# A three-stage layer kernel: the first wide layer as seven products of quarters, and both wide layers' weights loaded for every block

## The chip, the cores and the metric

The kernel runs on one core of one Trainium2 chip. The metric is the device time of one execution in microseconds (us), the median of three runs.

## What is computed

x has 4 sequences of 1024 tokens with 256 channels. Three sublayers follow each other, each of them behind a layer norm and added to its input: half a feed-forward net, a long convolution, and half the same feed-forward net again. Cut to what matters:

```python
def _L0_ffn_ref(x, w1_w, w1_s, w2_w, w2_s, h1_w, h1_s, h2_w, h2_s, w3_w, w3_s):
    h = silu(_tlin(x, w1_w, w1_s)) * _tlin(x, w2_w, w2_s)      # 256 -> 1024
    h = gelu(_tlin(h, h1_w, h1_s))                             # 1024 -> 1024, first wide layer
    h = gelu(_tlin(h, h2_w, h2_s))                             # 1024 -> 1024, second wide layer
    return _tlin(h, w3_w, w3_s)                                # 1024 -> 256
x = x + 0.5 * ffn(layernorm(x))
x = x + gelu(causal_convolution(layernorm(x), K)) @ W.T + b    # K: 1024 taps for each channel
x = x + 0.5 * ffn(layernorm(x))
```

`_tlin(x, w, s)` is x times the transpose of w, scaled by s for each output; all the weights w are -1, 0 or 1.

## The kernel before

**Blocks.** The 4096 tokens are cut into 8 blocks of 512. The feed-forward net runs over the 8 blocks as turn "f" (x to x1) and again as turn "g" (x2 to the output), 16 blocks in the order f0 to f7, g0 to g7. In between, the convolution takes each of the 4 sequences through `mix`, from x1 to x2. Activations lie with features on the 128 partitions and the block's 512 tokens along the free axis.

**Two parts.** Activations go to TensorE as fp32r in two parts, an upper part (a cast) and a lower part (value minus upper part), so each product is two matmuls. Weights are whole numbers and need one part. The program also looks at the weights on the chip (`weight_checks`, 44 pieces), and a second copy of the whole program in plain fp32 stands behind an `If` for weights that fp32r can't hold; it doesn't run here.

**A block's stages (`ffn`, L352).** First the narrow layer: for each of 8 groups of 128 features m, 4 matmuls for pa (w1) and 4 for pb (w2), then Silu on ScalarE (L362), the product on VectorE (L363), the cast on ScalarE (L367) and the low part on VectorE (`low_part`, L287). Then the two wide layers: for each m, 8 chunks k x 2 parts = 16 matmuls of 512 columns into one PSUM bank (`linear`, L344), Gelu (L377), cast (L379), low part (L287). Last, w3 with 32 matmuls: `last_squares` with an addition on GpSimd and stores by its queue, in the final block `last_tokens` (L423), whose 64 matmuls have 256 columns of w3 as the moving operand. A block has 352 fp32r matmuls, 256 of them in the wide layers.

**Buffers.** All weights are resident in SBUF; h1_sb and h2_sb take 32 KB of each partition each. The activations in two parts rotate through 15 "ring" buffers, other tiles of 512 columns through 19 "half" buffers, and all matmul results through 8 PSUM banks that share one tag.

**The order of the work.** A compile-time scheduler of the language sets each engine's order; the order of the code is the priority, and what is ready may go ahead. Convolution work is mixed into the blocks: `all_aside` is a generator for the kernel's taps, their spectrum and the four `mix`es, and after each m of a wide layer `tick` draws from it until about 2500 units are drawn, where a VectorE operation counts 130 plus its columns (L137). A generator step that yields PAUSE ends a tick, and where nothing is left, a tick takes a weight check instead. In parallel `ahead` steps `prepare` (L956), which loads, normalizes and transposes the next block. `spectrum` (L699) multiplies by trigonometric matrices that SP's queue loads (`matrix`, L713): products into PSUM, a copy by ScalarE (f_m, L731), sums and differences on VectorE. `mix` ends with the inverse (pi, L905), Gelu (yt) and the product with W (pw, L930).

**Queues.** At the start GpSimd's queue loads w1, w2, the tap parameters, h1, h2, the second block, w3 and the rest, in this order. SP's queue loads the first block, the constants, and later all that blocks and convolution read; GpSimd's stores.

Of the kernel before, what the change touches and what calls it, by code (L numbers as in the profile page):

```python
# [31 lines left out]
JQ = J // 2  # L32
N_WARM = 9


STEP_WORK, OP_WORK, MIN_WORK = 2500, 130, 300
PAUSE = "pause"
N_CHECKS = 44

# [58 lines left out]
def macaron_layers(  # L98
# [22 lines left out]

    nc = tc.nc
# [7 lines left out]
    psum = ctx.enter_context(tc.tile_pool(name="psum", bufs=8, space=bass.MemoryType.PSUM))  # L130

    work_done = 0
# [16 lines left out]
    def bank(name):  # L149
        return psum.tile([P, 512], F32, tag="ps", name=name)  # L150

    def half(name, *shape, dtype=F32):

        return work.tile([P, *(shape or (512,))], dtype, tag="half", name=name, bufs=19)

    def ring(name, *shape, dtype=F32):

        return work.tile([P, *shape], dtype, tag="ring", name=name, bufs=15)
# [9 lines left out]
    h1_sb = keep.tile([P, KH, HID], wide, name="h1_sb")  # L168
    h2_sb = keep.tile([P, KH, HID], wide, name="h2_sb")
# [12 lines left out]
    k_hat = dram.tile([2 + len(PAIRS), 2, P, 2, D], F32, name="k_hat")  # L182

# [37 lines left out]


# [21 lines left out]
    for t, src in ((h1_sb, h1), (h2_sb, h2)):  # L244
        for k in range(0, KH, 2):
            weights_from.dma_start(t[:, k : k + 2, :], rows(src)[:, k : k + 2, :])
# [42 lines left out]
    def transposed(xn, name):  # L289


        pts = [bank(f"pt_{name}_{k}") for k in range(DC)]
# [47 lines left out]
    def linear(ps, w, m, acts):  # L340
        n = len(acts)
        for k in range(n):
            for part in range(parts):
                nc.tensor.matmul(  # L344
                    ps,
                    w[:, k, m * P : (m + 1) * P],
                    acts[k][:, part, :],
                    start=(k == 0 and part == 0),
                    stop=(k == n - 1 and part == parts - 1),
                )  # L350

    def ffn(xt, src, dst, blk, name, tick, ahead, final):  # L352


        ha = []
        for m in range(KH):
            pa, pb = bank(f"pa_{name}_{m}"), bank(f"pb_{name}_{m}")
            linear(pa, w1_sb, m, xt)
            linear(pb, w2_sb, m, xt)
            g = half(f"g_{name}_{m}")  # L360
            t = ring(f"ha_{name}_{m}", parts, TB, dtype=wide)
# [4 lines left out]
            if split:  # L366
                nc.scalar.copy(t[:, 0, :], g)  # L367
                low_part(t, g)
            ha.append(t)
        for layer, w in ((2, h1_sb), (3, h2_sb)):  # L370
            hb = []
            for m in range(KH):
                ps = bank(f"p{layer}_{name}_{m}")
                linear(ps, w, m, ha)
                t = ring(f"h{layer}_{name}_{m}", parts, TB, dtype=wide)
                g = half(f"g{layer}_{name}_{m}") if split else t[:, 0, :]
                nc.scalar.activation(g, ps, AF.Gelu, scale=sc_sb[:, layer, m : m + 1])  # L377
                if split:
                    nc.scalar.copy(t[:, 0, :], g)  # L379
                    low_part(t, g)  # L380
                hb.append(t)
                ahead()
                if layer == 2 or m < KH - 1:
                    tick()
            ha = hb
# [3 lines left out]
        (last_tokens if final else last_squares)(ha, src, dst, blk, name)  # L389

    def last_squares(ha, src, dst, blk, name):
# [8 lines left out]
        for k in range(DC):  # L400
            ps = bank(f"po_{name}_{k}")
            linear(ps, w3_sb, k, ha)
# [7 lines left out]
    def last_tokens(ha, src, dst, blk, name):  # L410
# [7 lines left out]
        def result(ps, i, n):  # L418

            for e in range(n):  # L420
                for k in range(KH):
                    for part in range(parts):
                        nc.tensor.matmul(  # L423
                            ps[:, e * D : (e + 1) * D],
                            ha[k][:, part, (i + e) * P : (i + e + 1) * P],
# [18 lines left out]
        ps = bank(f"po_{name}_0")  # L444
# [3 lines left out]
        for e in range(2):  # L448
            ps = bank(f"po_{name}_{2 + e}")
# [5 lines left out]
    def weight_checks():  # L455

        todo = []
        for src, held in ((w1, w1_sb), (w2, w2_sb), (h1, h1_sb), (h2, h2_sb), (w3, w3_sb)):
            n_k, width = held.shape[1], held.shape[2]
            by = max(1, 512 // width)  # L460
            for k in range(0, n_k, by):
                for c in range(0, width, 512):
                    cols = slice(c, min(c + 512, width))
                    todo.append((rows(src)[:, k : k + by, cols], held[:, k : k + by, cols]))
        assert len(todo) == N_CHECKS

        def load(n):
            given = half(f"given_{n}", *todo[n][1].shape[1:])
# [5 lines left out]
        for n, (src, held) in enumerate(todo):  # L474
            given = following
            if n + 1 < len(todo):
                following = load(n + 1)
            stt(
                given,
                given,  # L480
                0.0,
                held.bitcast(F32),
                ALU.add,
                ALU.not_equal,
                accum_out=miss[:, n : n + 1],
            )
            yield

# [3 lines left out]
        nc.vector.tensor_reduce(total, miss[:, 0:N_CHECKS], axis=mybir.AxisListType.X, op=ALU.add)  # L492
        yield
        ps = psum.tile([1, 1], F32, tag="ps", name="p_bad")
# [109 lines left out]
    def kernel_steps():  # L604
# [7 lines left out]
        for g0 in range(0, DD, group):  # L612
# [34 lines left out]
            def products(d1, a):  # L647
# [3 lines left out]
                if at == 0:  # L651
                    pk = psum.tile([P, per_tile, 2, NB], F32, tag="ps", name=f"pk_{g0 + d1}")
# [46 lines left out]
    def spectrum(rows_of, name, over=1):  # L699
# [22 lines left out]
        def products(q, m):  # L722
            ps = []
            for e in range(2):
                ps.append(psum.tile([P, 2, D], F32, tag="ps", name=f"pf_{name}_{q}_{e}"))
# [17 lines left out]
        for n in (0, 2):  # L743
            qs = order[n : n + 2]
            if n == 0:
                for q, m in zip(qs, ms):
                    products(q, m)
                ms = [matrix(q) for q in order[2:4]]
                yield PAUSE
            for q in qs:  # L750
                sums(q)
            if n == 0:
# [369 lines left out]
```

## Time and profile before

| | |
|---|---|
| median of 3 runs | 1405.61 us (1404.97 to 1405.88) |
| profiled execution | 1405.23 us, its span 1403.3 us |
| granted TensorE clock | 0.999 |
| TensorE busy | 1393.0 us, 6492 matmul instructions |
| VectorE busy | 838.6 us (60%) |
| ScalarE busy | 707.6 us (50%), 51 table loads ahead of Gelu |
| DMA | 101.27 MB, mean 72 GB/s; 355 GB/s in the first 35 us |

In a group's line stand the line of the code, the engine, the operation, the written tile and those read, the shapes and the count; then the busy time and the mean time of one in ns, then the idle time ahead of it and what ended that. The timeline's lines begin with the start and the length in us. PEld is TensorE's weight load, which overlaps its matmuls. Two rows that the change touches:

```profile
L344 PE MATMUL p_g<-ha_g,h_sb 128*128 128x512 f32 x1024 | 236.2, 390 | 0.0
L287 DVE TENSOR_TENSOR h_g<-g_g,h_g 128x512 fp32r<-128x512 f32 x128 | 88.6, 692 | 249.6 <-ACT h_g L379 249.3
```

### The profile page before, as it was taken

How to read it: one execution, taken by the hardware profiler on the slowest of the kernel's cores; microseconds unless marked ns; L12 is line 12 of the kernel's file. 1: busy time of each engine (PE TensorE's matmuls, PEld its weight loads, DVE VectorE, ACT ScalarE, POOL GpSimd, SP SyncE). 2: the span in 40 equal slices, each digit the busy share in tenths (PEclk: the TensorE clock that was granted, in tenths of full speed). 3: DMA queues.
4: the chain of work that ended last, by engine and by line, in shares of the span. 5: the costliest groups of instructions: out<-in, count | busy, mean ns of one | idle time of the engine just before them, and what ended most of it. 6: DMA issues, size and time to landing. Idle time of an engine off the chain costs nothing.

```text
span 1403.3 us, 17882 instructions
## 1 busy us (share of the span) xinstructions
PE 1393.0 (99%) x6492; PEld 1161.4 (83%) x6492; DVE 838.6 (60%) x1614; ACT 707.6 (50%) x1070; POOL 266.3 (19%) x398
## 2 busy tenths in 40 slices
PE   8999999999999999999999999999999999999998
PEld 7888888888888888888888888888888888888887
DVE  6896567755547774387773568753566762542412
ACT  5986579644546344354352454533545342553532
POOL 4321012211312120320113201213112121121200
PEclk9999999999999999999999999999999999999999
DMA  9410101112231322422213404132223122511000
GB/s 355 117 20 26 35 16 46 30 48 77 67 96 30 113 71 73 136 60 84 61 53 113 113 31 138 20 97 74 86 70 82 43 63 98 135 22 39 15 16 19
DMA packets 111139, 101.27 MB, mean 72 GB/s; under 512 B 72304, under 2 KB 82544, under 8 KB 111040
## 3 DMA queue, kind: packets, MB, share of 16 engines
q1 hardware_dynamic: 93248, 55.37, 14.6%
q0 software_dynamic: 17520, 44.39, 11.1%
q8 instruction: 53, 0.87, 0.3%
q14 instruction: 46, 0.38, 0.1%
q10 hardware_dynamic: 272, 0.26, 0.1%
HBM read 76.91 MB, written 23.07 MB: 71 GB/s over the span
## 4 chain that ended last, share of the span: by engine, by line
PE 99%; DMA 1%; POOL 0%; DVE 0%; issue 0%; POOLq 0%
PE p_f L344 33%; PE p_g L344 33%; PE po_f L344 4%; PE pa_g L344 4%; PE pb_g L344 4%; PE pa_f L344 4%; PE pb_f L344 4%; PE po_g L344 4%; PE pi L905 2%; PE pf_m L727 2%; PE pw L930 2%; PE pk L654 1%; PE po_g L423 1%; DMA w_sb<-in_w_dram 1%; PE pf_k L727 0%; POOL w_sb L238 0%
## 5 line engine op out<-in xcount | busy, mean ns | idle before, releaser
L287 DVE TENSOR_TENSOR h_g<-g_g,h_g 128x512 fp32r<-128x512 f32 x128 | 88.6, 692 | 249.6 <-ACT h_g L379 249.3
L344 PE MATMUL p_f<-h_f,h_sb 128*128 128x512 f32 x1024 | 237.1, 391 | 0.0
L344 PE MATMUL p_g<-ha_g,h_sb 128*128 128x512 f32 x1024 | 236.2, 390 | 0.0
L344 PE MATMUL p_f<-ha_f,h_sb 128*128 128x512 f32 x1024 | 235.3, 390 | 0.0
L344 PE MATMUL p_g<-h_g,h_sb 128*128 128x512 f32 x1024 | 235.2, 390 | 0.0
L377 ACT ACTIVATE g_g<-p_g,sc_sb 128x512 f32<-128x512 f32 x128 | 88.2, 689 | 278.9 <-PE p_g L344 276.5
L344 PEld LDWEIGHTS p_g<-ha_g,h_sb 128*128 128x128 f32 x1024 | 192.1, 188 | 39.8
L344 PEld LDWEIGHTS p_g<-h_g,h_sb 128*128 128x128 f32 x1024 | 192.1, 188 | 39.8
L344 PEld LDWEIGHTS p_f<-h_f,h_sb 128*128 128x128 f32 x1024 | 191.8, 188 | 40.1 <-DVE h_f L287 0.3
L344 PEld LDWEIGHTS p_f<-ha_f,h_sb 128*128 128x128 f32 x1024 | 191.9, 188 | 39.8
L377 ACT ACTIVATE g_f<-p_f,sc_sb 128x512 f32<-128x512 f32 x128 | 87.7, 689 | 190.0 <-PE p_f L344 189.6
L287 DVE TENSOR_TENSOR h_f<-g_f,h_f 128x512 fp32r<-128x512 f32 x128 | 87.8, 690 | 149.0 <-ACT h_f L379 148.5
L317 POOL DMA_DIRECT2D moved<-sq_g x64 | 34.9, 552 | 330.3 <-DVE sq_g L140 290.7
L379 ACT CAST h_g<-g_g 128x512 fp32r<-128x512 f32 x128 | 79.3, 620 | 4.0
L379 ACT CAST h_f<-g_f 128x512 fp32r<-128x512 f32 x128 | 78.3, 618 | 2.9
L377 ACT ACT_TABLE_LOAD x51 | 65.4, 1283 | 26.0 <-PE p_f L344 14.3
L344 PE MATMUL pa_f<-xt_f,w_sb 128*128 128x512 f32 x256 | 69.0, 390 | 1.1 <-DVE xt_f L299 0.7
L344 PE MATMUL pb_f<-xt_f,w_sb 128*128 128x512 f32 x256 | 68.8, 389 | 0.0
L344 PE MATMUL pa_g<-xt_g,w_sb 128*128 128x512 f32 x256 | 68.4, 389 | 0.0
L344 PE MATMUL pb_g<-xt_g,w_sb 128*128 128x512 f32 x256 | 68.4, 389 | 0.0
L363 DVE SCALAR_TENSOR_TENSOR g_g<-pb_g,sc_sb,g_g 128x512 f32<-128x512 f32 x64 | 47.9, 749 | 31.5 <-PE pb_g L344 19.7
L317 POOL DMA_DIRECT2D moved<-sq_f x56 | 30.8, 556 | 181.2 <-DVE sq_f L140 181.2
(234 smaller groups left out, 1844.4 us busy)
## 6 DMA issues: line engine op xcount, KB each, us to landing
h_sb<-in_h_dram POOLq DMA_DIRECT2D x8, 1024.0 KB, 15.0
given<-in_h_dram SPq DMA_DIRECT2D x32, 256.0 KB, 3.6
kr<-k_hat SPq DMA_DIRECT2D x20, 256.0 KB, 2.6
ki<-k_hat SPq DMA_DIRECT2D x20, 256.0 KB, 2.8
xr_f<-in_x_dram SPq DMA_DIRECT2D x64, 64.0 KB, 2.4
x<-y_f POOLq DMA_DIRECT2D x64, 64.0 KB, 2.2
xm<-x SPq DMA_DIRECT2D x8, 512.0 KB, 3.7
m_m<-in_cosm_dram SPq DMA_DIRECT2D x16, 256.0 KB, 5.2
```

Of the source, the lines that this page charges most:

```text
L287: return nc.vector.tensor_tensor(t[:, 1, :], src, t[:, 0, :].bitcast(F32), ALU.subtract)
L317: stores.dma_start(moved[k].rearrange("(c r) a q -> a r c q", r=SQ)[a], sq[a * SQ : (a + 1) * SQ].rearrange("r c j s -> r c (j s)"),)
L344: nc.tensor.matmul(ps, w[:, k, m * P : (m + 1) * P], acts[k][:, part, :], start=(k == 0 and part == 0), stop=(k == n - 1 and part == parts ...
L363: nc.vector.scalar_tensor_tensor(g if split else t[:, 0, :], pb, sc_sb[:, 1, m : m + 1], g, ALU.mult, ALU.mult)
L377: nc.scalar.activation(g, ps, AF.Gelu, scale=sc_sb[:, layer, m : m + 1])
L379: nc.scalar.copy(t[:, 0, :], g)
L423: nc.tensor.matmul(ps[:, e * D : (e + 1) * D], ha[k][:, part, (i + e) * P : (i + e + 1) * P], w3_sb[:, k, :], start=(k == 0 and part == 0) ...
L654: nc.tensor.matmul(pk[0:NA, at + i, :, :].rearrange("p h b -> p (h b)"), a[:, i].rearrange("p a b -> p (a b)"), qd[d1 // per_tile][:, at + ...
L727: nc.tensor.matmul(ps[e][:, part, :], m[:, e, part, :], rows_of(q + JQ * e), start=True, stop=True)
L905: nc.tensor.matmul(banks[dc][e][:, q * P : (q + 1) * P], vs[q + JQ * e][:, part, dc * P : (dc + 1) * P], m[:, e, part, :], start=(part == ...
L930: nc.tensor.matmul(ps[:, e * D : (e + 1) * D], yts[dc][j // JQ][:, (j % JQ + e) * P : (j % JQ + e + 1) * P], wt_sb[:, dc, :], start=(dc == 0),
```

## The change

**Seven products.** In all blocks but f0, the first wide layer is computed as a two-by-two product of quarters: the weights in four quarters of 512 x 512 (A), the activations in four quarters of 512 features x 256 tokens (B), with seven products of quarters and sums of quarters (Winograd's form of Strassen's method) in place of eight. The sums of weights (S1, S2, S3, S4, -A22) are made once, during f0, and stored in DRAM beside A11 and A12. The sums of activations (t1 to t4), the additions of kept products (p1, p5, u2) and the low parts are VectorE's; casts, copies out of PSUM and Gelus are ScalarE's. A product is 32 matmuls of 256 columns over two PSUM banks.

**Weights in quarters.** h1_sb and h2_sb are gone. Four slots of 1 MB take quarters: seven for the first wide layer and four for the second, in every block, on SP's queue. h2 is copied from DRAM to DRAM at the start (and quarters A11 and A12 of h1), f0's h1 quarters come by GpSimd's queue.

**What goes with it.** PSUM is divided: six banks with tags of their own for the net, two for the convolution. Ring has 14 buffers, half 18. Ticks come in the narrow layer too (1700 units after every second m), after each bank of a product (600) and after each m of a plain wide layer (3100). `spectrum` goes through its four products one by one with a PAUSE each, its matrices loaded two ahead; the inverse does its two halves of two banks each with a PAUSE between. The checks of h1 and h2 take two VectorE passes each instead of one and look at the weights in DRAM.

```diff
+NARROW_WORK, SUMS_WORK, WIDE_WORK = 1700, 600, 3100
+ORDER = (A11, S1, A12, S2, S3, S4, MINUS_A22)
...
-    psum = ctx.enter_context(tc.tile_pool(name="psum", bufs=8, space=bass.MemoryType.PSUM))
+    psum = ctx.enter_context(tc.tile_pool(name="psum", bufs=1, space=bass.MemoryType.PSUM))
...
+    def piece(name, tag):
+        return work.tile([P, TB], F32, tag=tag, name=name, bufs=5)
...
+                t = work.tile([P, QK, QW], F32R, tag="slot", name=f"w_f0_0_{m}{k}", bufs=4)
+                weights_from.dma_start(t, quarter_of(h1, m, k))
+        nc.sync.dma_start(h2_raw, h2)
+        nc.sync.dma_start(quarters[A11], quarter_of(h1, 0, 0))
+        nc.sync.dma_start(quarters[A12], quarter_of(h1, 0, 1))
...
+            if split and m % 2 == 0:
+                tick(NARROW_WORK)
+        if by_sums:
+            acts = winograd(raw, name, tick, ahead)
+        for layer in (3,) if by_sums else (2, 3):
+            acts = plain(acts, layer, name, tick, ahead)
...
+    def operand(quarter, name):
+        ops = []
+        for p, src in enumerate(quarter):
+            t = ring(f"{name}_{p}", parts, TB, dtype=wide)
+            nc.scalar.copy(t[:, 0, :], src)
+            low_part(t, src)
+            ops.append(t)
+        return ops
...
+    def product(banks, weights, ops, step, first=True):
+        for p, ps in enumerate(banks):
+            for e in range(2):
+                m = 2 * p + e
+                for c in range(QK):
+                    for part in range(parts):
+                        nc.tensor.matmul(
+                            ps[:, e * QT : (e + 1) * QT],
+                            weights[:, c, m * P : (m + 1) * P],
+                            ops[c // 2][:, part, c % 2 * QT : (c % 2 + 1) * QT],
...
+            step()
...
+        def times(banks, ops, first):
+            product(banks, slots.pop(0), ops, step, first)
+            load_slot()
...
+        def plus(sums, banks):
+            for o, ps in zip(sums, banks):
+                nc.vector.tensor_tensor(o, ps, o, ALU.add)
+            return sums
+
+        def activated(k, n, quarter, into):
+            for p, (src, g) in enumerate(zip(quarter, into)):
+                for c in range(2):
+                    m = k * QK + 2 * p + c
+                    cols = slice(c * QT, (c + 1) * QT)
+                    nc.scalar.activation(
+                        g[:, cols], src[:, cols], AF.Gelu, scale=sc_sb[:, 2, m : m + 1]
+                    )
+                upper, lower = (t[:, :, n * QT : (n + 1) * QT] for t in out[2 * k + p])
+                g = g.rearrange("p (c t) -> p c t", c=2)
+                nc.scalar.copy(upper, g)
+                nc.vector.tensor_tensor(lower, g, upper.bitcast(F32), ALU.subtract)
+
+        b11 = operand(of(0, 0), named("b11"))
+        t1 = less(of(0, 1), of(0, 0), named("t1"))
+        t1_ops = operand(t1, named("t1s"))
+        times(pa, b11, True)
+        p1 = kept(pa, named("p1"))
+        t2 = less(of(1, 1), t1, named("t2"))
+        t2_ops = operand(t2, named("t2s"))
+        times(pd, t1_ops, True)
+        p5 = kept(pd, named("p5"))
+        b21 = operand(of(1, 0), named("b21"))
+        times(pa, t2_ops, False)
+        u2 = kept(pa, named("u2"))
+        t3 = less(of(1, 1), of(0, 1), named("t3"))
+        t3_ops = operand(t3, named("t3s"))
+        times(pe, b21, True)
+        activated(0, 0, plus(p1, pe), p1)
+        b22 = operand(of(1, 1), named("b22"))
+        times(pa, t3_ops, False)
+        activated(1, 1, plus(p5, pa), p5)
+        t4 = less(t2, of(1, 0), named("t4"))
+        t4_ops = operand(t4, named("t4s"))
+        times(pd, b22, False)
+        activated(0, 1, plus(u2, pd), u2)
+        times(pa, t4_ops, False)
+        activated(1, 0, pa, [piece(f"c21_{name}_{p}", "sum") for p in range(2)])
...
+        t = work.tile([P, QK, QW], F32R, tag="slot", name=name, bufs=4)
+
+        nc.sync.dma_start(t.bitcast(F32), src)
+        slots.append(t)
```

`less` makes two differences on VectorE ("diff" pieces), `kept` two copies out of PSUM on ScalarE ("sum" pieces), and `pa`, `pd`, `pe` are the net's bank pairs 4 and 5, 0 and 1, 2 and 3. `load_slot` fetches the next quarter in the order of use.

## The prediction

> **What bounds the kernel now.** I read the busy table and the chain that ended last first, then TensorE's groups by form, then one stage in the timeline.
>
> ```profile
> PE 1393.0 (99%) x6492; PEld 1161.4 (83%) x6492; DVE 838.6 (60%) x1614; ACT 707.6 (50%) x1070; POOL 266.3 (19%) x398
> ...
> PE 99%; DMA 1%; POOL 0%; DVE 0%; issue 0%; POOLq 0%
> PE p_f L344 33%; PE p_g L344 33%; PE po_f L344 4%; PE pa_g L344 4%; PE pb_g L344 4%; PE pa_f L344 4%; PE pb_f L344 4%; PE po_g L344 4%; PE pi L905 2%; PE pf_m L727 2%; PE pw L930 2%; PE pk L654 1%; PE po_g L423 1%; DMA w_sb<-in_w_dram 1%; PE pf_k L727 0%; POOL w_sb L238 0%
> ```
>
> TensorE is the whole chain, and the two wide layers (p_f, p_g) are two thirds of it. Its waits, listed, come to 3.9 us, all in the first 11 us. So time falls only if TensorE gets less work, and rises as soon as TensorE has to wait.
>
> What a matmul costs is read from start to start, since the ends overlap. TensorE's timeline, a whole wide layer and the last layer of the last block, and the weight loads of the latter:
>
> ```profile
> 715.76 29.18 PE L344 MATMUL p_g<-ha_g,h_sb 128*128 128x512 f32 x128
> 744.78 1.05 PE L905 MATMUL pi<-mi,v_False 128*128 128x128 f32 x8
> ```
> ```profile
> 1388.83 8.09 PE L423 MATMUL po_g<-w_sb,h_g 128*128 128x256 f32 x64
> 1391.14 5.57 PEld L423 LDWEIGHTS po_g<-w_sb,h_g 128*128 128x128 f32 x46 [0.20 <-DVE h_g L287]
> ```
>
> (744.78 - 715.76) / 128 = 226.7 ns for 512 columns. L423 is the only place where fp32r matmuls have 256 columns, each with its own weight load, and that is the form the change makes: the undisturbed 46 take (5.57 - 0.19) / 45 = 119.6 ns. That is 6 ns over half of 226.7: each matmul carries some 13 ns that don't shrink with its columns.
>
> **The products.** Per block, the first wide layer's 128 matmuls of 512 columns (29.02 us) become 7 products x 4 row groups x 4 chunks x 2 parts = 224 of 256 columns: 224 x 119.6 = 26.79 us. The saving is 2.23 us, not the eighth (3.63 us) that the algebra has. Block f0 keeps the old form, so 15 x 2.23 = **33.4 us** off the path.
>
> Here the Trainium skill ("TensorE: Matmul & The Clock Gate", section Back-to-back issue gap) is weighed. It puts a sustained stream of weight load and matmul at 81 ns for 128 columns and 131 ns for 512, which speaks against the change: between those, 256 columns would be about 98 ns (my interpolation), so 224 x 98 = 22.0 us against 128 x 131 = 16.8 us, a loss of 5.2 us a block and 78 in all. The trace excludes its 131: it has 226.7 here. Its formula for one isolated matmul, N/2.4 + 2.5 ns, gives 27.6 - 24.5 = 3.2 us a block, 47 in all. I take the rows of the trace, between the two.
>
> **VectorE.** Of the block's low-part subtractions, 16 fall away (8 ha_, 8 of the first wide layer). The sums bring 14 low parts of operands, 8 differences, 6 additions of kept products and 8 low parts of results: 36, net +20. All have forms the trace has:
>
> ```profile
> 728.83 0.68 DVE L140 TENSOR_TENSOR v_False<-u_i,w_i 128x512 f32<-128x512 f32 x1
> 729.43 0.68 DVE L140 TENSOR_TENSOR v_True<-u_i,w_i 128x512 f32<-128x512 f32 x1
> ```
>
> Each lasts 0.68 but the next starts after 0.60 us. So 36 x 0.60 = 21.6 us lie in the seven-product stage, where 8 low parts (4.8 us) lie today. Over the run: 15 x 20 x 0.60 = 180 us, plus 16 sums of weights (10 us), plus one more pass for each of 32 weight checks (19 us): 838.6 + 209 = 1048 us, some 75% of a span near 1386. By the average it is covered. By stage less so: the stage gets 14 ticks of 600 units of spectrum work; 642 units are one 512-column op of 0.60 us, so up to 7.9 us. 21.6 + 7.9 = 29.5 us of VectorE if the budget is used fully, 26.7 at the two thirds that I estimate (about 410 us of counted work against 16 x 37,500 units, 560 us), beside TensorE's 26.8 plus its own spectrum work. That (pf, pw, pi, pk: 28.9 + 28.9 + 33.8 + 16.4 = 108 us, 7 a block) gives the stage some 1.6 us. So 28.4 against 26.7 to 29.5: VectorE just fits, because the six ops for b11 and t1 (3.6 us) need only the first half of the narrow layer.
>
> They may run that early because engines don't follow the code's order:
>
> ```profile
> 704.18 0.75 DVE L363 SCALAR_TENSOR_TENSOR g_g<-pb_g,sc_sb,g_g 128x512 f32<-128x512 f32 x1 [1.29 <-ACT g_g L362]
> 705.16 0.75 DVE L363 SCALAR_TENSOR_TENSOR g_g<-pb_g,sc_sb,g_g 128x512 f32<-128x512 f32 x1 [0.23 <-PE pb_g L344]
> 705.83 1.71 DVE L287 TENSOR_TENSOR ha_g<-g_g,ha_g 128x512 fp32r<-128x512 f32 x2
> ```
>
> The code has product, low part, product, low part; the program has two products, then two low parts. What is ready goes first, so operands of later products fill gaps.
>
> **ScalarE** per block loses 16 casts (0.62 each) and 8 Gelus (0.69), 15.4 us; it gains 14 + 8 casts (13.6), 6 copies from PSUM (0.59, the row f_m: 3.5) and 16 Gelus of 256 columns (about 0.41, by the 256-column row k_minus: 6.6), 23.7 us. Net 8.3 x 15 = 125 us; 707.6 becomes 832, 60%. Hidden by the average.
>
> **The new waits.** Which comes last in the stage? The "sum" tag has five buffers; kept p1, p5 and u2 want six. So the second piece of u2 waits for p1's first piece, and product 5, which adds into u2's bank, waits for u2's copy. In us from the stage's start, at 3.83 a product: product 4's first bank ends at 13.4; 0.24 until another engine sees it (19.39 streamed, ScalarE at 19.63 in the 715.8 stage); addition 0.69; the Gelu table 1.28; two Gelus 0.82; cast 0.62; low part 0.69; copy 0.59: 18.3. Product 5's second bank wants to start at 17.2. TensorE would wait 1.1 us, more by each op queued ahead on two engines near 90% in this stage, less where product 6 (which needs none of this) or spectrum matmuls are placed in the gap. Bounds: 0 when filled; 2 to 4.5 us when ScalarE's order is late. I take 0.8: **15 x 0.8 = 12 us**. The other tight place, the second wide layer's start, needs product 6's results: addition, Gelus, cast, low part make 3.1 us after its last bank, and product 7 covers 3.83. Without that cover it costs up to 3.1 us a block.
>
> **Weights.** Each block now loads 11 quarters of 1 MB on SP's queue, where nothing was loaded: about 169 MB more. A slot is reused four products on, so a load has three products, 11.5 us. 256 KB land in 2.6 to 3.6 us and 512 KB (xm) in 3.7, so I estimate 5.5 for 1 MB. In the stage 7 MB in 28 us is 250 GB/s, beside 46 to 93 GB/s there now; the start shows 355 GB/s as what the engines move. Near full, but two of the seven aren't needed until the next layer's second half. Cost 0, bound 2 us a block. Queued behind a slot load that waits for TensorE are SP's loads for the spectrum (m, mi, xr, factors); the diff loads matrices two products ahead, so I take 0.
>
> **The start.** The first 35 us are already full:
>
> ```profile
> 0.00:35.00 35.00, 31.11 (x138) 25.80 (x139) 23.59 (x56) 19.45 (x30) 14.95 (x27) 1.00 1.10 355
> ```
>
> (TensorE, weight loads, VectorE, ScalarE, GpSimd, clock, DMA share, GB/s.) SP now copies 6 MB from DRAM to DRAM at once, beside w1 and w2, for which TensorE waits until 10.47. At half the bandwidth their second chunks, issued at 3.2 and landing after 7.2 us, would come up to 7 us later; the h1 quarters then still arrive in time at 7.2 us each. I take **4 us** (0 to 7). The weight sums (4 MB read, 5 written) come in f0's ticks and are due at its end: 0.
>
> **Other moves.** The spectrum's PSUM goes from eight shared banks to two: after each pair a copy (0.59) and two sums (1.2) must pass. Wide matmuls fill that, as the 64 pi matmuls lie between them today; 0, bound 1 us a block. h1_sb and h2_sb gone, 14 ring buffers in place of 15, GpSimd's extra 20 stores in f0: 0. The checks fit the ticks of the last blocks, where VectorE is 2 to 5 tenths busy.
>
> **Sum** against the profiled execution (1405.23 us; span 1403.3; median of the runs 1405.61, 0.03% away): 1405.2 - 33.4 + 12 + 4 = **1388 us**.
>
> **Rivals.**
> *Nothing waits:* 1405.2 - 33.4 + 4 = 1376. For it: 22 of the 36 sums make operands, which can be done early. Chance 0.13.
> *The stage turns on ScalarE and VectorE (slower).* From product 4's first bank to the next layer's start 13.4 us, ScalarE has three activations of 2.9 us, the table 1.28, the b22 and t4 casts and the u2 copy 3.1: 13.1 us. The next block's norm falls there (Sqrt 0.3 with its table, then Gelu's again: 2.9 us). That is 16.0, so products 5 to 7 come late. At 4.5 us a block: 1405.2 - 33.4 + 4 + 67.5 = 1443. It decides from (33.4 - 4) / 15 = 1.96 us a block. Against it: the norm and the b22 and t4 casts (2.5) can be drawn earlier. Chance 0.30.
> *256 columns cost more.* All 64 of L423 with its waits are 8.09 / 64 = 126 ns; then 28.3 us a product stage, 12 us saved, and 1409 with the costs above. Chance 0.08.
> *Even:* the quarters or half the late chain eat 2 us a block: 1405. Chance 0.07.
> *The forecast,* 1377 to 1401: 0.42.
>
> Faster by over 0.2% (2.8 us, about what a measurement can tell from no change): 0.42 + 0.13 = 0.55; within it 0.07; slower 0.38. The range leaves a tenth at each end: 1373 to 1442.
>
> **What would show it.** The product matmuls start 119 to 121 ns apart: the first step. VectorE near 75% overall, over 85% in the stage: the second. TensorE's waits before the products: 0.8 us a block on ScalarE's copy (u2) in products 5 or 6; if they name the b22 or t4 low parts or the outputs at the next layer's start, and sum to 30 us or more, the slower rival holds. Waits on the quarters' DMA prove my zero wrong. The first wide matmul after 24.2 tells the start.

## The result and the profile after

The change made the kernel slower: 1520.21 us (median of 4 runs, 1517.22 to 1523.28) against 1405.74 us; ratio 1.0815, 95% interval 1.0792 to 1.0838. The forecast was 1388 us. The profiled execution's span is 1519.2 us. Its page, in the lines that answer to those of before:

```profile
PE 1411.8 (93%) x7932; PEld 1231.3 (81%) x7932; DVE 1062.3 (70%) x1963; ACT 817.1 (54%) x1373; POOL 277.1 (18%) x414
...
PEclk7999999999999999999999999999999999999999
...
PE 42%; DVE 6%; DMA 3%; issue 1%; ACT 1%; SPq 0%; POOL 0%; DVEq 0%; ACTq 0%; POOLq 0%
```

VectorE and ScalarE are near the forecast sums (1048 and 832 us). TensorE is not: it stands idle for 107 us of the span (10 before). Whom it waited for, the longest first (total us, times, longest):

```profile
PE p2a_g L531 <- ACT u_g L550: 15.2, 7, 3.9
PE p2a_f L531 <- ACT u_f L550: 12.8, 6, 3.0
PE pb_f L385 <- DMA w_sb<-in_w_dram: 12.7, 1, 12.7
PE pa_f L385 <- ACT g_f L417: 8.2, 1, 8.2
PE p2a_f L531 <- DVE b_f L328: 7.5, 3, 3.4
PE p2d_g L531 <- DVE t1s_g L328: 5.1, 3, 2.9
```

The first two are the wait for u2's copy, the next two are the start, the last two the first operands b11 and t1. None of them was there before.

Where did 115.9 us of span come from? I cut TensorE's timeline of both kernels into stages and summed, for each, its length, the time in which TensorE was idle, and (1 - granted clock) times the length, called the slow clock's share:

| | before, us | after, us | waits in it | slow clock |
|---|---|---|---|---|
| block f0, narrow layer | 15.4 | 43.1 | 23.6 | 13.8 |
| block f0, the rest | 65.5 | 78.9 | 8.1 | 2.4 |
| 15 blocks, first wide layer | 493.4 | 523.4 | 53.3 | 23.7 |
| 15 blocks, all else | 813.8 | 858.0 | 12.7 | 6.3 |

Block f0 gives 41.1 us, and 0.5 lies ahead of its first matmul. In its narrow layer the two last columns overlap, since the clock was low during the waits too: TensorE was busy 19.5 us there, where it was busy 14.9 before. The other 15 blocks give 74.2: 33.4 us less work, but 66.0 us of waits and 30.0 us of slow clock; 11.6 us remain. (Spectrum work moved from the wide into the narrow layers, so the stages compare only in sum.)

A quiet block, g7, that has no spectrum work, shows the stage bare. Of its seven products, the fourth and the fifth in TensorE's timeline (the weights come as A11, S1, S2, A12, S3, S4, -A22):

```profile
1456.51 4.00 PE L531 MATMUL p2e_g<-b_g,w 128*128 128x256 f32 x32
...
1460.35 2.08 PE L531 MATMUL p2a_g<-t3s_g,w 128*128 128x256 f32 x16
...
1464.56 3.65 PE L531 MATMUL p2a_g<-t3s_g,w 128*128 128x256 f32 x16 [2.12 <-ACT u_g L550]
```

Product 4 (p2e) takes 1460.35 - 1456.51 = 3.84 us for 32 matmuls, 120 ns each: the forecast's 119.6. Then the second half of product 5 (p2a with t3s) waits 2.12 us for u2, and the same 16 matmuls that took 2.08 us in the first half take 3.65. The stretches tell why (length, TensorE, weight loads, VectorE, ScalarE, GpSimd, granted clock, DMA share, GB/s): product 4; product 5 with its wait; and, cut more finely, the 3.41 us in which the wait lies and the 3.41 us after them.

```profile
1456.50:1460.30 3.80, 3.80 (x34) 3.80 (x33) 0.69 (x1) 1.09 (x3) 0.00 (x0) 1.00 0.75 272
1460.30:1468.00 7.70, 5.58 (x34) 5.37 (x34) 3.88 (x6) 5.11 (x10) 0.00 (x0) 0.79 0.46 166
...
1461.33:1464.74 3.41, 1.29 (x11) 1.08 (x10) 1.89 (x3) 3.23 (x7) 0.00 (x0) 1.00 0.81 282
1464.74:1468.15 3.41, 3.41 (x17) 3.41 (x17) 1.29 (x2) 1.83 (x4) 0.00 (x0) 0.50 0.10 32
```

The clock was 0.79 over these 7.7 us: 1.00 up to the end of the wait, then 0.50 for 3.41 us. So a quiet stage lasts 30.83 us where it lasted 29.02, and should have lasted 26.9 (224 x 120 ns).

### The profile page after: what moved, and what is told of

Same layout as the page of the kernel before. It is cut to its first block, busy times and chain, and to the rows that moved or that the text cites. A ratio compares the mean times of both kernels' runs of the same rounds, so it can differ in the third digit from the quotient of the medians.

```text
span 1519.2 us, 21747 instructions
## 1 busy us (share of the span) xinstructions
PE 1411.8 (93%) x7932; PEld 1231.3 (81%) x7932; DVE 1062.3 (70%) x1963; ACT 817.1 (54%) x1373; POOL 277.1 (18%) x414
## 4 chain that ended last, share of the span: by engine, by line
PE 42%; DVE 6%; DMA 3%; issue 1%; ACT 1%; SPq 0%; POOL 0%; DVEq 0%; ACTq 0%; POOLq 0%
PE p_g L445 13%; PE p2a_g L531 7%; PE p2d_g L531 4%; PE pa_g L385 3%; PE pb_g L385 3%; PE po_g L385 3%; PE p_f L445 2%; PE p2e_g L531 2%; PE pw L1226 1%; PE pi L1200 1%; PE pf_m L1025 1%; DMA ki<-k_hat 1%; DMA m_m<-in_cosm_dram 1%; PE p2a_f L531 1%; DVE g_g L418 1%
## 5 line engine op out<-in xcount | busy, mean ns | idle before, releaser
L445 PE MATMUL p_f<-h_f,w 128*128 128x512 f32 x1024 | 239.3, 392 | 2.9 <-DVE h_f L328 2.8
L445 PE MATMUL p_g<-h_g,w 128*128 128x512 f32 x1024 | 237.3, 391 | 0.0
L445 PEld LDWEIGHTS p_f<-h_f,w 128*128 128x128 f32 x1024 | 190.9, 188 | 43.4 <-DVE h_f L328 4.0
L445 PEld LDWEIGHTS p_g<-h_g,w 128*128 128x128 f32 x1024 | 192.0, 188 | 39.5
L456 ACT ACTIVATE g_g<-p_g,sc_sb 128x512 f32<-128x512 f32 x64 | 44.1, 689 | 138.2 <-PE p_g L445 107.5
L358 POOL DMA_DIRECT2D moved<-sq_g x64 | 34.9, 552 | 320.4 <-DVE sq_g L152 319.4
L385 PE MATMUL pb_f<-xt_f,w_sb 128*128 128x512 f32 x256 | 72.9, 403 | 14.7 <-DMA w_sb<-in_w_dram 12.7
L385 PEld LDWEIGHTS pb_f<-xt_f,w_sb 128*128 128x128 f32 x256 | 49.3, 194 | 26.9 <-DMA w_sb<-in_w_dram 13.0
L385 PEld LDWEIGHTS pa_f<-xt_f,w_sb 128*128 128x128 f32 x256 | 49.7, 196 | 24.6 <-ACT g_f L417 8.7
L418 DVE SCALAR_TENSOR_TENSOR g_f<-pb_f,sc_sb,g_f 128x512 f32<-128x512 f32 x64 | 47.3, 743 | 31.3 <-PE pb_f L385 26.2
L385 PE MATMUL po_f<-h_f,w_sb 128*128 128x512 f32 x256 | 63.5, 399 | 4.0 <-DVE h_f L328 3.0
L385 PEld LDWEIGHTS po_f<-h_f,w_sb 128*128 128x128 f32 x256 | 48.0, 191 | 17.3 <-DVE h_f L328 5.5
```

Of the source, the lines that this page charges most:

```text
L358: stores.dma_start(moved[k].rearrange("(c r) a q -> a r c q", r=SQ)[a], sq[a * SQ : (a + 1) * SQ].rearrange("r c j s -> r c (j s)"),)
L385: nc.tensor.matmul(ps, w[:, k, m * P : (m + 1) * P], acts[k][part], start=(k == 0 and part == 0), stop=(k == n - 1 and part == parts - 1),)
L418: nc.vector.scalar_tensor_tensor(g if split else t[:, 0, :], pb, sc_sb[:, 1, m : m + 1], g, ALU.mult, ALU.mult)
L445: nc.tensor.matmul(ps, w(k, m), acts[k][part], start=(k == 0 and part == 0), stop=(k == KH - 1 and part == parts - 1),)
```

## The experiments

**Theory.** Three losses that add up: the fifth buffer for kept products (u2's wait and the clock behind it), the start, and late first operands in busy blocks. **Rival.** VectorE and ScalarE set the stage's pace, so that a wait that is taken away comes back at the next operand.

**1. Six buffers for kept products (e_sum6).**

```diff
-        return work.tile([P, TB], F32, tag=tag, name=name, bufs=5)
+        return work.tile([P, TB], F32, tag=tag, name=name, bufs=6 if tag == "sum" else 5)
```

> Only change against the changed kernel: six buffers for the kept products (tag sum) in place of five, so that the second piece of u2 no longer waits for p1's first piece. My theory: the wait for u2's copy (28 us in the profile) goes, and with it the slow clock behind it (about 1.7 us in each of 13 blocks, 22 us): about 1470 us. Rival, VectorE and ScalarE set the stage's pace: the wait only moves to the low parts of b22 and t4 or to the next layer's start, and the time stays above 1500 us.

Measured: 1499.7 us (ratio to before 1.0674, 1.0656 to 1.0691). A gain of 20 us, not 50. The u2 waits are gone, but others are new, 16.7 us, all for product 6's operand b22. The larger ones:

```profile
PE p2d_g L531 <- DVE b_g L328: 5.7, 6, 1.5
PE p2d_f L531 <- ACT b_f L512: 5.0, 3, 3.3
...
PE p2d_f L531 <- DVE b_f L328: 3.3, 5, 0.9
```

The rival has a part: the next late thing stood 1 us behind. But is it VectorE's load or only its order? In the quiet block of the changed kernel VectorE idles 4.75 us in the middle of the stage, and b22's low parts come after that:

```profile
1458.63 0.69 DVE L582 TENSOR_TENSOR p_g<-p2e_g,p_g 128x512 f32<-128x512 f32 x1 [4.75 <-PE p2e_g L531]
...
1465.05 1.29 DVE L328 TENSOR_TENSOR b_g<-g_g,b_g 128x512 fp32r<-128x512 f32 x2 [0.62 <-ACT b_g L512]
```

**2. The start (e_start): copies last in GpSimd's list, sums of weights after the first narrow layer.**

```diff
-        nc.sync.dma_start(h2_raw, h2)
-        nc.sync.dma_start(quarters[A11], quarter_of(h1, 0, 0))
-        nc.sync.dma_start(quarters[A12], quarter_of(h1, 0, 1))
...
     weights_from.dma_start(bias_sb, bias.partition_broadcast(P))
+    if split:
+        weights_from.dma_start(h2_raw, h2)
+        weights_from.dma_start(quarters[A11], quarter_of(h1, 0, 0))
+        weights_from.dma_start(quarters[A12], quarter_of(h1, 0, 1))
...
-        next(sums_of_weights, None)
+        if ticks > 4:
+            next(sums_of_weights, None)
```

> Only change: the three copies from DRAM to DRAM are issued last in GpSimd's list of loads in place of first on SP's queue, and the sums of weights begin after the first narrow layer. My theory: the first narrow layer ends near 26 us in place of 52.5, and the later part of block f0 is no worse: about 1490 us. Rival: the 14 us that f0 loses after its narrow layer are the price of the weight sums and will be larger when they are later; then 1500 us or more.

Measured: 1509.3 us (1.0743, 1.0725 to 1.0760). f0's narrow layer fell from 43.1 to 19.0 us and ended at 28.0, near the 26 expected, but the rest of f0 rose from 78.9 to 88.3. The rival is nearer.

**3. Both (e_both).** The edits of 1 and of 2 together:

```diff
+        return work.tile([P, TB], F32, tag=tag, name=name, bufs=6 if tag == "sum" else 5)
...
+        weights_from.dma_start(h2_raw, h2)
...
+        if ticks > 4:
+            next(sums_of_weights, None)
```

> Six sum buffers and the late copies together. My theory, in which the two losses are independent: about 1440 us (1520 less 50 less 30). What is left above the 1376 of the sum without waits are the late operands in the blocks that carry much spectrum work. Rival (the stage's pace is set by VectorE and ScalarE): 1475 us or more.

Measured: 1487.5 us (1.0578, 1.0561 to 1.0596). 20.5 + 10.9 = 31.4 us expected from the two alone, 32.7 measured: they are independent, but each is smaller than I had it. In a quiet block the stage is 28.3 us, and product 6 waits 0.89 for b22 with no slow clock after it (30 matmuls in 3.86):

```profile
1433.73 3.86 PE L532 MATMUL p2d_g<-b_g,w 128*128 128x256 f32 x30 [0.89 <-DVE b_g L329]
```

**4. b22 and t4 ahead of the first activation (e_order).** As e_both, and in the code:

```diff
+        b22 = operand(of(1, 1), named("b22"))
         times(pe, b21, True)
+        t4 = less(t2, of(1, 0), named("t4"))
+        t4_ops = operand(t4, named("t4s"))
         activated(0, 0, plus(p1, pe), p1)
-        b22 = operand(of(1, 1), named("b22"))
         times(pa, t3_ops, False)
         activated(1, 1, plus(p5, pa), p5)
-        t4 = less(t2, of(1, 0), named("t4"))
-        t4_ops = operand(t4, named("t4s"))
```

> As e_both (six sum buffers, late copies), and in the code b22 and t4 stand ahead of the first activation, so that their casts and low parts have the higher priority. My theory: the waits of product 6 for b22 (16.5 us in e_both) go, the stage of a quiet block falls from 28.3 to 27.4 us; about 1468 us. Rival (VectorE has no time left in the stage): the waits come back at the other operands or at the next layer, 1480 us or more.

Measured: 1462.2 us (1.0392, 1.0370 to 1.0415). In the middle of the stage it was order, not load: 25 us are gained by moving lines. The quiet stage has no wait left and lasts 26.9 us, 2.1 less than before the change. The products 5 to 7 now follow each other at 3.84 us:

```profile
1407.32 4.00 PE L532 MATMUL p2a_g<-t3s_g,w 128*128 128x256 f32 x32
1411.15 4.00 PE L532 MATMUL p2d_g<-b_g,w 128*128 128x256 f32 x32
1414.99 4.00 PE L532 MATMUL p2a_g<-t4s_g,w 128*128 128x256 f32 x32
1418.84 21.50 PE L446 MATMUL p_g<-h_g,w 128*128 128x512 f32 x94
```

What is left in this stage over 15 blocks is 19.1 us of waits, 18.3 of them for b11 and t1 in busy blocks, and 11.8 of slow clock.

**5. The clock (e_fill).** The changed kernel, with useless work in place of the wait: 16 more matmuls in product 5, behind its first bank, and one column of their result copied away.

```diff
+            if fill and p == 0:
+                spare = bank("spare")
+                for i in range(16):
+                    nc.tensor.matmul(
+                        spare[:, 0:QT],
+                        weights[:, i % QK, 0:P],
+                        ops[0][:, i % 2, 0:QT],
...
+                nc.vector.tensor_copy(unread, spare[:, 0:1])
...
-        times(pa, t3_ops, False)
+        times(pa, t3_ops, False, True)
```

> The changed kernel with 16 more matmuls of 256 columns between the two banks of product 5, whose result isn't used (VectorE reads one column of it): 1.9 us of useless work in the place of the 2.1 us wait for u2. If it is the wait alone that costs, the time stays at 1520 us. If TensorE's clock falls by half after a wait of that length and costs as much again, a quiet block's stage falls from 30.8 to about 29.1 us and the time to about 1500 us, though TensorE does more.

Measured: 1514.2 us (1.0767, 1.0749 to 1.0785), 6 us less although TensorE does 15 x 1.92 = 29 us more. In the quiet block:

```profile
1461.05 2.08 PE L544 MATMUL spare<-t3s_g,w 128*128 128x256 f32 x16
1463.34 2.18 PE L531 MATMUL p2a_g<-t3s_g,w 128*128 128x256 f32 x16 [0.21 <-ACT u_g L562]
```

The second half of product 5 takes 2.18 in place of 3.65, the stage 29.9 in place of 30.8. Over 15 blocks the stage's waits fell from 53.3 to 30.7 us and the slow clock's share from 23.7 to 11.9. So the clock's halving behind a wait of 2 us costs nearly as much again as the wait. The gain is less than expected: in the changed kernel the stage's clock is below 1.00 in 10 of the 15 blocks, not in all.

**6. The rearrangement without the seven products (e_plain8, and its ticks, PSUM and copies).** Eight products in every block, quarters loaded for both layers:

```diff
-        by_sums = split and name != "f0"
+        by_sums = False
```

> The first wide layer as eight products (plain, in every block), all else as in the changed kernel: quarters loaded for every block (h1 as well, from a copy), PSUM divided, ticks, spectrum. No sums of weights; the copies are late in GpSimd's list. It tells what the loads and the rearrangement cost without the seven products. My theory: nearly nothing, 1405 to 1415 us. Rival, the 11 (here 8) MB for each block and the divided PSUM delay TensorE: 1430 us or more, with TensorE's waits named by a DMA of w or by the spectrum's products.

Measured: 1450.1 us (1.0319, 1.0300 to 1.0338): 44 us that have nothing to do with seven products. 13 of them lie in f0, 10 there waiting for the late copy of h2 that this experiment itself brought. In the last five blocks, which have no spectrum work, a block's stages are 14.54, 29.14, 29.01 and 7.25 us (the last one's 8.09), 0.16 in sum above the kernel before: there the loads cost next to nothing. The other 31.6 us lie almost wholly in the blocks with spectrum work.

> As e_plain8, with ticks as before: none in the narrow layer, 2500 units after each group of the wide layers. If spectrum work in the narrow layer, where VectorE already has the products, is what costs e_plain8 its waits there, it falls to about 1425; if not, it stays within 5 us of 1450.

```diff
-NARROW_WORK, SUMS_WORK, WIDE_WORK = 1700, 600, 3100
+NARROW_WORK, SUMS_WORK, WIDE_WORK = 0, 0, 2500
```

Measured: 1433.6 us (1.0208, 1.0191 to 1.0225), 16 us less. In the profiled executions the 15 blocks after f0 fell from 1338.8 to 1319.7 us, against 1307.2 before, but the profiled one of e_plain8_ticks was its fastest, 5.5 us below the median. So these ticks cost some 16 us. The edit also lowers the wide layers' ticks from 3100 to 2500, so how much the narrow layer's ticks alone cost is not separated.

> As e_plain8 (eight products), with all eight PSUM banks shared again as in the kernel before. If the divided PSUM is what costs e_plain8 its 32 us outside the first block, it falls to about 1420; if not, it stays within 5 us of 1450.

```diff
-        return psum.tile([P, 512], F32, tag="ps", name=name, bufs=2)
+        return psum.tile([P, 512], F32, tag="ps", name=name, bufs=8)
...
-        return psum.tile([P, 512], F32, tag=f"ffn{i % 6}", name=name)
+        return psum.tile([P, 512], F32, tag="ps", name=name, bufs=8)
```

Measured: 1446.3 us (1.0284, 1.0267 to 1.0301). The divided PSUM costs about 4 us here; with the seven products no run tells.

The ticks of e_plain8_ticks, and h2's copy in GpSimd's list ahead of the late loads (x_second), in halves:

```diff
-NARROW_WORK, SUMS_WORK, WIDE_WORK = 1700, 600, 3100
+NARROW_WORK, SUMS_WORK, WIDE_WORK = 0, 0, 2500
...
+    if split:
+        for m in range(2):
+            weights_from.dma_start(h2_raw[:, m * QW : (m + 1) * QW], h2[:, m * QW : (m + 1) * QW])
...
-        weights_from.dma_start(h2_raw, h2)
```

> As e_plain8_ticks (eight products, ticks as before), with h2's copy ahead of the second block's and w3's loads, so that block f0's second wide layer no longer waits for it (8 us and the slow clock after it). It leaves the loads of quarters and the divided PSUM as the only differences in the steady blocks. If loading 8 MB for each block is free: 1415 to 1422 us; if not, it stays at 1430.

Measured: 1432.2 us (1.0205, 1.0177 to 1.0234). By its figure that is the rival's 1430, but this one misses its aim: f0 waits elsewhere now (9.2 us for ScalarE in its second wide layer) and loses 14.8 us. The other 15 blocks, 1317.8 us, are within 11 us of before. Why these 11 remain, where only 3.5 us of waits are seen, is open, and with it a small cost of the loads.

**7. The weight sums (e_nosums).** As e_order, without the sums: the five quarters that should hold them are copies of quarters of h1.

```diff
+        for i in (S1, S2, S3, S4, MINUS_A22):
+            weights_from.dma_start(quarters[i], quarter_of(h1, 1, i % 2))
...
-        if ticks > 4:
-            next(sums_of_weights, None)
```

> As e_order without the sums of weights: the five quarters that hold sums are copies of quarters of h1 (so the first wide layer is another one), made at the end of GpSimd's list. It tells what the sums (4 MB read, 5 MB written, 16 VectorE operations, ScalarE's four, all within block f0) cost. If they make block f0's 27 us, it falls to about 1445 us; if f0's loss is the ticks in its narrow layer and the divided PSUM, to 1455 or not at all.

Measured: 1442.5 us (1.0270, 1.0253 to 1.0287), 20 us less than e_order; f0 falls from 108.7 to 85.1 us (80.9 before). The sums of weights, which I had priced at nothing, cost 20 us once.

**8. Where the spectrum's work goes (e_order_budget, e_low, e_mid), and GpSimd (e_pool, e_low_pool).** All as e_order, and the ticks, in this order e_order_budget, e_low, e_mid:

```diff
-NARROW_WORK, SUMS_WORK, WIDE_WORK = 1700, 600, 3100
+NARROW_WORK, SUMS_WORK, WIDE_WORK = 850, 0, 4800
...
+NARROW_WORK, SUMS_WORK, WIDE_WORK = 800, 300, 3100
...
+NARROW_WORK, SUMS_WORK, WIDE_WORK = 1300, 400, 3700
```

> As e_order, with the spectrum's work moved out of the stage: ticks of 850, 0 and 4800 units in place of 1700, 600 and 3100 (37,000 a block in place of 36,900). If VectorE's load in the narrow layer and the stage is what delays the first operands (b11, t1: 17 us of waits in e_both), these go: about 1445 us. If the spectrum's work then crowds the second wide layer, its results are late for the last layer and the time stays at 1465 to 1475.

Measured: 1502.1 us (1.0680, 1.0662 to 1.0698). Neither figure was met. The stage fell to 421 us over 15 blocks, with 9.3 us of waits and no slow clock. But the last layer rose from 117.5 to 165.3: its operands, the second wide layer's results, are late.

```profile
PE po_f L386 <- ACT h_f L436: 17.8, 5, 7.8
PE po_f L386 <- DVE h_f L329: 13.3, 9, 5.1
```

> As e_order, with less of the spectrum's work in the narrow layer and in the stage and no more in the second wide layer: ticks of 800, 300 and 3100 units (29,100 a block in place of 36,900). If the first operands (b11, t1) are late only because spectrum work stands ahead of them on VectorE, their 18 us of waits go and the time falls to about 1435. If the work that is put off comes back (mixes late for the second turn, or crowded later blocks), 1455 to 1475.

Measured: 1543.2 us (1.0982, 1.0964 to 1.1001). The stage is 416 us with 1.2 us of waits: with fewer ticks the first operands come in time. But the work comes back, at a higher price than expected: a mix is late for the second turn, and the weight checks aren't done when the last block ends.

```profile
PE p_bad L792 <- DVE total L789: 41.2, 1, 41.2
PE pi L1201 <- DVE v_False L152: 34.3, 2, 25.7
```

> As e_order with ticks of 1300, 400 and 3700 units (36,700 a block, as many as 36,900 but between e_order's and e_order_budget's places). If VectorE is full in one place or the other whatever the place, it lies between 1460 and 1500 us; if there is a place for the spectrum's work where the seven products don't wait, 1440 us.

Measured: 1459.9 us (1.0375, 1.0346 to 1.0404): 2.3 us below e_order's 1462.2, which is within the spread of the two. The stage gained 31 us, the other stages and f0 lost as much.

GpSimd for t2, t3, t4 (t1 stays on VectorE) and for the four sums of each piece of weights (e_pool):

```diff
-    def less(a, b, name):
+    def less(a, b, name, on=nc.gpsimd):
...
-            nc.vector.tensor_tensor(o, x_, y_, ALU.subtract)
+            on.tensor_tensor(o, x_, y_, ALU.subtract)
...
-            nc.vector.tensor_tensor(s1, a[1, 0], a[1, 1], ALU.add)
+            nc.gpsimd.tensor_tensor(s1, a[1, 0], a[1, 1], ALU.add)
...
```

> As e_order, with the differences t2, t3, t4 and the sums of weights on GpSimd (1.3 us each in place of 0.6): VectorE is rid of 54 us of the run, 3.6 us a stage. If VectorE's load is what is left of the loss, about 1440 us, and block f0 some 8 us shorter. If GpSimd's slower pass only makes t2 and its successors late, 1462 us or more.

Measured: 1494.3 us (1.0630, 1.0613 to 1.0648), 32 us more; f0 is 4 us longer, not 8 shorter. VectorE does 106 instructions less and yet is busy 10 us longer (1073.7 for 1063.7). The low parts of the g blocks' operands, e_order first, then e_pool:

```profile
L329 DVE TENSOR_TENSOR b_g<-g_g,b_g 128x512 fp32r<-128x512 f32 x48 | 37.6, 805 | 0.4 <-ACT b_g L513 0.4
```
```profile
L329 DVE TENSOR_TENSOR b_g<-g_g,b_g 128x512 fp32r<-128x512 f32 x48 | 50.6, 1082 | 0.2 <-ACT b_g L513 0.2
...
L522 POOL TENSOR_TENSOR t_g<-g_g,t_g 128x512 f32<-128x512 f32 x16 | 34.3, 2147 | 41.1 <-DVE g_g L419 29.4 <-DVE t_g L522 11.7
```

The means mix two cases. Of e_pool's 90 low parts of b operands (f and g), 60 overlap no addition or subtraction of GpSimd and take 0.67 to 0.69 us; the 30 that do take 1.62 on the mean. In e_order 11 of 90 overlap one. GpSimd's own operations take 1.30 us on the mean in the kernel before (additions) and between 1.5 and 2.1 here (t2, t3 and t4). So the two slow each other, and moving work to GpSimd didn't free VectorE. The two moves, differences and sums of weights, were not tried apart.

The ticks of e_low with e_pool's edits (e_low_pool):

```diff
-NARROW_WORK, SUMS_WORK, WIDE_WORK = 1700, 600, 3100
+NARROW_WORK, SUMS_WORK, WIDE_WORK = 800, 300, 3100
...
+    def less(a, b, name, on=nc.gpsimd):
```

> Both: less spectrum work in the stage and three of the differences on GpSimd. If VectorE is the cause, this is the fastest form of the seven products, 1420 to 1430 us, still above the kernel before because of the weight sums in f0 and the spectrum's ticks. Rival: 1455 or more, if put-off work comes back.

Measured: 1587.5 us (1.1297, 1.1269 to 1.1326). A clear miss: the losses of e_low (81 us above e_order) and of e_pool (32) add up, and 12 us more.

No form tried beats the kernel before. The best complete form of the seven products is e_mid or e_order, 54 to 56 us above it.

## Why the prediction was wrong, point by point

**The step that failed** is the sum's costs, not its saving. Against the 33.4 us saved stood 12 for TensorE's waits in the stage and 4 for the start; the clock, the first operands, the sums of weights and the loads queued behind the quarters stood at nothing: 16 us in all. The profiled execution has 77.0 us of waits and slow clock in the stage, 41.6 in f0 and ahead of it, and 19.0 in the other stages.

**What bounds the kernel, and the products: right.** 120 ns a matmul was forecast from the 46 matmuls of L423 and measured; in e_order the quiet stage is 26.88 us, 2.14 less than 29.02 (2.23 forecast).

**The new waits: right place, wrong size.** The wait for u2 was found ahead from the buffer count and priced at 0.8 us a block, with 2 to 4.5 as its upper bound. It was 28.0 us in 13 blocks, 1.9 on the mean of 15, and e_sum6 removes it. The chain to u2's copy was to end 18.3 us into the stage; in the quiet block it ends after 19.5, since both engines had other work ahead in their order (ScalarE's cast and copy, VectorE's addition and low parts):

```profile
1461.70 0.60 ACT L595 CAST h_g<-p_g 128x512 fp32r<-128x512 f32 x1
...
1463.92 0.58 ACT L550 COPY u_g<-p2a_g 128x512 f32<-128x512 f32 x1
```
```profile
1462.54 0.69 DVE L582 TENSOR_TENSOR p_g<-p2a_g,p_g 128x512 f32<-128x512 f32 x1 [1.29 <-PE p2a_g L531]
1463.15 1.28 DVE L596 TENSOR_TENSOR h_g<-p_g,h_g 128x512 fp32r<-128x512 f32 x2
```

The cast of p1's first piece stands behind a Gelu of its second piece, which starts at 1461.28, and the low part of the first piece behind the addition for product 5's first bank, which waits for that bank. And product 6 didn't fill the gap: its operand b22, which stands behind the first activation in the code, wasn't ready either. The gap ends at 1464.56, b22's low parts start at 1465.05 (shown at e_sum6). What is ready goes first only among what the order lets become ready. No run has b22 early with five buffers, so whether product 6 would then have filled the gap is not shown.

**The clock: left out of the sum.** I priced waits at their own length. With e_fill's filling in place of the u2 wait the stage's slow clock is 12 us less; in all 15 blocks its share was 30 us.

**VectorE just fits: right as a sum, wrong in time.** A stage held 27.2 us of VectorE's work on the mean (26.7 to 29.5 forecast), and its total was right to 14 us (1062 for 1048). But b11 and t1, which were to be made in the first half of the narrow layer, come late in busy blocks: 17.9 us of waits under b_f, b_g, t1s_g and g_f. Their code stands behind the narrow layer's ticks of 1700 units, which I had costed at nothing. In block f2 the cast of b11's second piece ends at 230.97 and its low part starts at 238.60, behind seven operations of the ticks, four of the narrow layer's own and a difference on VectorE. e_low, with fewer units drawn, has hardly any such wait. e_order_budget, e_low and e_mid show that shifting that work shifted the loss too. That VectorE has no place for 20 more operations of 0.6 us in the busy blocks is my reading, and not shown: no run puts b11 and t1 ahead of the narrow layer's ticks, as e_order did with b22 and t4 in the middle of the stage.

**Weights: right as far as the runs show; the loads behind them: wrong.** A quarter lands after 5.0 to 5.2 us (5.5 estimated), and TensorE waits for none outside f0. But the spectrum's loads, queued behind the slots' loads, were also taken at 0, and TensorE waits 4.9 us for one of them, a matrix (m_m) in g0's second wide layer. SP issued it at 848.6, right after a quarter's load for which it had waited from 838.2 to 847.6, and it landed 11 us later.

**The start: mis-sized by a factor of seven.** 4 us forecast (0 to 7); f0's narrow layer lost 27.7. The first chunk of w2 landed 20.0 us after its issue in place of 4.0, the second chunks of w1 and w2 after 22.8 and 25.4 in place of 7.2 and 8.4: SP's 6 MB of copies, issued from 2.2 to 3.5 us, shared the DMA with them, and loads of h1 pieces followed. In e_start, with the copies late, these three take 6.1, 8.9 and 10.2 us. TensorE's start shows the waits for the first two of these, the next wait, and half speed after it:

```profile
22.60 0.79 PE L385 MATMUL pb_f<-xt_f,w_sb 128*128 128x512 f32 x1 [12.72 <-DMA w_sb<-in_w_dram]
26.04 0.80 PE L385 MATMUL pa_f<-xt_f,w_sb 128*128 128x512 f32 x1 [2.65 <-DMA w_sb<-in_w_dram]
...
41.95 2.07 PE L385 MATMUL pa_f<-xt_f,w_sb 128*128 128x512 f32 x4 [8.24 <-ACT g_f L417]
```

The third wait, 8.24 us on Silu, was a queue that I had not walked: ScalarE's negation of a piece of h1 stood ahead of the Silu and waited for VectorE's first sum, which waited for the piece to land; VectorE's timeline and ScalarE's show it.

```profile
38.53 0.69 DVE L659 TENSOR_TENSOR s<-a,a 128x512 f32<-128x512 f32 x1 [27.89 <-DMA a<-in_h_dram]
39.26 0.63 ACT L660 ACTIVATE a<-a 128x512 f32<-128x512 f32 x1 [29.93 <-DVE s L659]
...
41.20 0.69 ACT L417 ACTIVATE g_f<-pa_f,sc_sb 128x512 f32<-128x512 f32 x1
```

Moved later, the sums cost 20 us all the same (e_nosums). f0 was VectorE's fullest block before, too (82% busy).

**The rivals.** "Nothing waits" is out. The slower one had 4.5 us a block for the stage, and waits and slow clock there came to (53.3 + 23.7) / 15 = 5.1. That is luck: its sign was 30 us or more of waits for b22, t4 or the outputs at the next layer's start, and in the changed kernel these come to 6 us, all for t4. It had ScalarE full with 16.0 of 13.4 us; ScalarE was busy for 22.1 us of a stage of 34.9 on the mean, and e_order's quiet stage runs without a wait. Its total of 1443 us also missed 37 us at the start and in f0, and the ticks.

Two slips in the prediction's working don't change this: 256 columns at 126 ns save 0.7 us a block, so 11 us and not 12; and 410 us of 560 are 73%, not two thirds, which makes VectorE's stage 27.4 us and not 26.7.

In one sum: 1403.3 - 33.4 + 77.0 (stage) + 19.0 (waits and clock in the other stages of 15 blocks) + 41.6 (f0 and ahead) + 11.6 = 1519.1, the span being 1519.2. The 11.6 are what is left over: TensorE is busy longer than the count of its matmuls gives. e_plain8 has as much (31.6 us less 16.5 of waits and 3.4 of slow clock). Its cause is open.

## What to carry to other kernels

Where an engine is the chain at 99%, a change that removes 2% of its work has to be read as a change of what it may wait for: the wait of 2.12 us lengthened the quiet stage by 3.95 us (30.83 against 26.88), so one a block is more than the saving here (2.14). Count buffers against the values that live at once, and for a gap that other work should fill, look in the order of the code whether that work can be ready by then; moving two operand computations up was worth 25 us. Work that runs once is priced in the block in which it runs, by that block's fullest engine and by every queue that it stands in, and not by the average. Operands that are to be made early have to stand early in the order.

## What was not expected of the hardware

TensorE's clock fell to half behind a wait of 2.12 us (16 matmuls in 3.65 us in place of 2.08) and not behind one of 0.89 us. The clock record in the changed kernel's trace says more. Its 16 low stretches in the 15 blocks last 3.41 us (one of them 6.83) and all start at whole multiples of 3.41 us from each other. If the time is cut there into pieces of 3.41 us, each piece at full clock in which TensorE is idle for 1.89 us or more is followed by one at half clock, 16 in all, and none with 1.82 us or less is. So where a wait lies counts: 2.12 us within one piece halved the clock, while 2.31 us in f4 and 2.91 in g4, which lie across two pieces, did not. In twelve of the experiments, cut in the same way, the border is less sharp: pieces with 1.5 to 1.8 us idle went both ways.

GpSimd's additions and subtractions and VectorE's low parts slow each other when they overlap: 0.68 to 1.62 us on VectorE, 1.3 to between 1.5 and 2.1 us on GpSimd. Loads of 1 MB beside dense matmuls did not slow these: in e_order's quiet stage the seven products take 3.84 us each, the first at 6 GB/s of DMA and the others at 225 to 281.
